# A four-layer image network: when the second layer's Toeplitz matrices are written, which queue loads half of each row tile, and where the next tile is normalized

## The chip, the cores and the metric

The kernel runs on one core of one Trainium2 chip. The metric is the device time of one execution in microseconds (us). Before the change the median of three runs was 6182.19 us (6163.62 to 6187.67).

The engines are named as the profile names them: PE is TensorE (PEld its weight loads), DVE is VectorE, ACT is ScalarE, POOL is GpSimd, SP is SyncE. SP computes nothing here; it issues DMAs. POOL issues DMAs too, among other work. A name with a q (SPq) is an engine's queue of such instructions.

## The reference

An image batch of 8 x 56 x 56 pixels with 192 channels goes through four layers, each with a normalization ahead of it and a residual sum after it. The first two layers are alike and are the ones that the change touches:

```
p = silu(x @ p_w.T + p_b)          # 192 -> 576 channels
q = silu(x @ q_w.T + q_b)
v = silu(x @ v_w.T + v_b)
a1 = rpe_mlp_1(positions) * decay  # one number for each lag and channel
a2 = rpe_mlp_2(positions) * decay
qv = q * v
o1 = toeplitz(qv along the width, a1)
o2 = toeplitz(qv along the height, a2)
y  = (p * (o1 + o2)) @ o_w.T + o_b # 576 -> 192
```

`toeplitz` is a causal and anticausal convolution of 56 positions: for each channel a 56 x 56 matrix whose entry depends on the difference of row and column alone. The third layer is a 7 x 7 depthwise convolution with a two-matrix MLP, the fourth is attention in windows.

## The kernel before, in words

All arithmetic is in float32. The eight samples are taken in pairs (j and j+4 stand together in a tile of 128 partitions), and the pairs in two halves, j0 = 0 and j0 = 2. For each Toeplitz layer and half there are three generators of work, which yield a planned time after each piece:

- `tno_qv` (called Q) projects 128 tokens at a time to q and v (matmuls, L256), adds the bias (DVE, L265), applies Silu (ACT, L275), multiplies (DVE, L278), and stores qv to DRAM through SP (L281). Each group of 256 tokens is loaded two groups ahead (L233) and normalized on ACT (L239). 128 tokens make three pieces of 5.3, 5.3 and 1.3 planned us.
- `tno_toeplitz` (called TZ) does the Toeplitz products. It goes through 18 numbers n = (block of 64 channels, direction d). For each n it loads a tile `q` of qv and a tile `tm` of matrices (L338), both two ahead. For d = 0 the load of `q` comes in two halves, each 56 partitions by 56 rows of 512 bytes (L328); for d = 1 it is one load of long rows (L331). Then come eight groups of products (`along`, L350 on PE, copied from PSUM by ACT at L357) and eight groups of transposes (`turned`, L367 on PE, copied or added by DVE at L370 and L373), and the sum goes to DRAM through POOL (L383). A yield comes after every four groups.
- `tno_out` (called O) does the gate p, the output projection and the residual. It has 28 steps of 224 tokens. A step runs on PE for two tiles at once: the p projection of the tile `now` and the output projection of the tile `before`. Its PSUM tiles are two for the gate (`gs`) and one named `P`, which holds the output projection and, in the same banks, the gate's last 64 channels (`rem`). [...] After the matmuls, ACT applies Silu to `gs` (L511), DVE adds bias and residual out of `P` (L521, L524), POOL stores the result (L117), ACT applies Silu to `rem` (L528), and DVE normalizes the tile `after` for the next step (L449, three instructions). The next step begins with L538, which multiplies by the gates.

`weave` runs a lane of one or two generators and takes pieces of another one between them, in proportion to planned time. When 0.9 of a generator's planned time is done, it calls for the first piece of the next one, which starts its loads; if that next one stands in the next lane, it first gives out all that is left of the pieces taken beside. The lanes are these, and the wall times are read from the profile:

| lane | pieces beside | us |
|---|---|---|
| Q of layer 0, j0 = 0 | matrices of layers 0 and 1 | 0 to 457 |
| Q of layer 0, j0 = 2 | TZ of layer 0, j0 = 0 | 457 to 1108 |
| O of layer 0, j0 = 0; Q of layer 1, j0 = 0 | TZ of layer 0, j0 = 2 | 1108 to 2062 |
| O of layer 0, j0 = 2; Q of layer 1, j0 = 2 | TZ of layer 1, j0 = 0 | 2062 to 3000 |
| O of layer 1, j0 = 0 | TZ of layer 1, j0 = 2 | 3000 to 3560 |
| O of layer 1, j0 = 2 | first half of the depthwise convolution | 3560 to 4190 |

The Toeplitz matrices are made by `expand_tables`: 36 copies for each layer from a small table in DRAM to the 56 x 56 matrices in DRAM, each copy 2048 rows of 224 bytes, issued by SP (L201). They read the table with an overlapping pattern, so that each row is the last one shifted by a position. The first lane begins with 20 of its yields already spent, since `first` is advanced by 20 before the second half's statistics are taken.

In the lanes of TZ the order of instructions on PE, ACT and DVE is the program's order. In the first lane and in the last one a scheduler orders them. SP and POOL take their DMAs in order, and one that has to wait holds up those behind it.

Of the kernel before, what the change touches and what calls it, by code (L numbers as in the profile page):

```python
# [21 lines left out]
B, H, W, C = 8, 56, 56, 192  # L22
# [16 lines left out]
class Net:  # L39
# [275 lines left out]
    def tno_toeplitz(self, j0, mats, qv, o):  # L315
# [3 lines left out]
        nc, p = self.nc, self.tz  # L319
        PR = H // 2  # L320

        def load(n):
            blk, d = divmod(n, 2)
            q = p.tile([128, H, 128], F32, name="q", bufs=2)
            if d == 0:
                for half in range(2):
                    of = qv[2 * blk + half, :T].rearrange("(h w) e -> w h e", w=W)
                    nc.sync.dma_start(q[64 * half : 64 * half + W], of)  # L328
            else:
                of = qv[2 * blk : 2 * blk + 2].rearrange("n (h w) e -> (n h) (w e)", w=W)  # L330
                nc.sync.dma_start(q.rearrange("p i e -> p (i e)"), of)  # L331
            return q
# [60 lines left out]
        for n in range(NS):  # L393
            blk, d = divmod(n, 2)
            q = loaded.pop(0)
# [23 lines left out]
    def tno_out(self, L, j0, xs, gn, o, ys, gn_next, early):  # L419
# [3 lines left out]
        nc, p, inp = self.nc, self.tp, self.inp  # L423
# [22 lines left out]
        def normalize(j, x):  # L446
            xn = p.tile([128, 3, N], F32, name="t4")
            for k in range(3):
                nc.vector.tensor_scalar(  # L449
                    xn[:, k, :], x[:, k, :], gn[:, j, k, 0:1], gn[:, j, k, 1:2], ALU.mult, ALU.add  # L450
                )
            return xn

        def step(now, before, after):
            if now:
                xn, s = now[5], now[3]
# [50 lines left out]
            if now:  # L507
                for i in range(2):
                    pg = p.tile([128, 2, 2, N], F32, name="t4")
                    for c in range(2):  # L510
                        nc.scalar.activation(  # L511
                            pg[:, c],
                            view(gs[i], c * 256, [[512, 2], [1, N]]),
                            AF.Silu,
                            bias=pb[:, 2 * i + c : 2 * i + c + 1],
                        )
                    gates.append(pg)
            if before:
                j, t, x, g, st, _ = before
                y = g[:, 0:3]  # L520
                nc.vector.scalar_tensor_tensor(  # L521
                    y[:, 0:2], P[:, :, :N], ob[:, 0:1], x[:, 0:2], ALU.add, ALU.add
                )
                nc.vector.scalar_tensor_tensor(y[:, 2], po2, ob[:, 1:2], x[:, 2], ALU.add, ALU.add)  # L524
                self.store_pair(ys, j, slice(t * N, (t + 1) * N), y)
            if now:
                pg = p.tile([128, N], F32, name="t1", bufs=1)
                nc.scalar.activation(pg, rem, AF.Silu, bias=pb[:, 4:5])  # L528
                gates.append(pg)
            return normalize(*after) if after else None  # L530

        gates = []

# [18 lines left out]
        if early:  # L552
            yield None
            xn = normalize(j0, x2[:, :, :N])
        yield 0.0
        if not early:
            xn = normalize(j0, x2[:, :, :N])
        done = None
        for n, (j, t) in enumerate(tiles):
# [9 lines left out]
            after = None  # L569
            if n + 1 < len(tiles):  # L570
# [6 lines left out]
                after = tiles[n + 1][0], x2[:, :, at : at + N]  # L577
            xn = step(now, before, after)
# [36 lines left out]
            pass  # L615

    @staticmethod
    def part(gen, t):

        for dt in gen:  # L620
            yield dt
            t -= dt
            if t <= 0:
                return

    def tno_layers(self, x0, x1, x2, gn, last):


        tc, nc = self.tc, self.nc
        LS = ("L0", "L1")  # L630
        tables = [

            [self.dram.tile([D1 + 1, 112], F32, name=f"{L}_tab{d}") for d in range(2)]
            for L in LS
        ]
        mats = [
            [self.dram.tile([D1 // 32, 64, 32 * H], F32, name=f"{L}_mat{d}") for d in range(2)]
            for L in LS
        ]
# [6 lines left out]
        with ExitStack() as ctx, ExitStack() as wqp:  # L646
# [5 lines left out]
            QT, OT, TZT = 25 * 2.25 * 5.3, 28 * 10.7, 8 + 72 * 3.2  # L652

            with tc.tile_pool(name="tab", bufs=2) as tab:
                self.input_stats(x0, gn[0], 0, tab)
                self.decay_tables("L0", tab, tables[0])
                first = Q(0, 0)
                for n in range(20):
                    next(first)
                self.input_stats(x0, gn[0], 2, tab)  # L660
                none = tab.tile([112, 512], F32, name="none", bufs=1)
                nc.gpsimd.memset(none, 0.0)
                for qv in qvs.values():
                    to = qv[:, T:].rearrange("n (p k) e -> p n (k e)", p=112)
                    nc.gpsimd.dma_start(to, view(none, 0, [[0, D1 // 32], [1, 512]]))
                self.decay_tables("L1", tab, tables[1])
                for t in tables:
                    for d in range(2):
                        nc.gpsimd.dma_start(t[d][D1:], none[:1, :112])
                lanes = [[(first, QT)], [(Q(0, 2), QT)], [(O(0, 0), OT), (Q(1, 0), QT)]]  # L670
                lanes += [[(O(0, 2), OT), (Q(1, 2), QT)], [(O(1, 0), OT)], [(O(1, 2, False), OT)]]
                mat = (m for i in range(2) for m in self.expand_tables(tables[i], mats[i]))
                self.weave(lanes[0], mat, lanes[1][0][0], 72.0, 0.0, 0.88)
            in_order = tc.manual_schedule(engines=ENGINES)
            with tc.tile_pool(name="tz", bufs=1) as self.tz, in_order:
                self.tms = []
# [909 lines left out]
```

## Time and profile before

| | us |
|---|---|
| median of three runs | 6182.19 |
| the profiled execution | 6174.82 |
| its span, first to last instruction | 6172.7 |
| PE busy | 5666.5 (92%) |
| weight loads of PE busy | 4464.1 (72%) |
| DVE busy | 2847.8 (46%) |
| ACT busy | 2153.0 (35%) |
| POOL busy | 639.2 (10%) |

Shares of busy time are means over stages. The profile gives for each wait who waited, at which line, and which instruction ended the wait: "PE bank L467 <- DVE t L449" means that PE at line 467, which writes the PSUM tile `bank`, stood idle until DVE at line 449 had written `t`. "issue" is idle time for which the profile shows no wait. In the timeline each line has the start, the length from there to the end of the merged group, the engine, the line, the operation, what it writes and reads, its shape, and how many instructions are merged; a bracket holds the idle time of the engine ahead of it and who ended it.

### The profile page before, as it was taken

The numbers are of one execution on the slowest core, as the hardware profiler recorded it, in microseconds if no ns is written. First come the engines' busy times: TensorE is split into PE (matmuls) and PEld (weight loads), VectorE is DVE, ScalarE is ACT, GpSimd is POOL, SyncE is SP. The second block draws the span as 40 slices with busy tenths as digits, with TensorE's granted clock in tenths as the row PEclk, the third lists the DMA queues.
The fourth block names the chain that finished last, engine by engine and source line by source line (L and its number), as shares of the span: only waits on it lengthen the run. The fifth ranks groups of instructions, "written<-read, shape, count | busy, mean of one in ns | idle before, by whom it ended". The sixth has DMA issues, their size and how long they took to land.

```text
span 6172.7 us, 151914 instructions
## 1 busy us (share of the span) xinstructions
PE 5666.5 (92%) x68832; PEld 4464.1 (72%) x68832; DVE 2847.8 (46%) x4858; ACT 2153.0 (35%) x2736; POOL 639.2 (10%) x833
## 2 busy tenths in 40 slices
PE   4997999899999999999889989999999999988997
PEld 3776878788778788888778878885665444666666
DVE  6663555444556444456444443242221322556555
ACT  1343444223444333344333332224323333333332
POOL 0000000000000000000000010000000100333332
PEclk9998999999999999999999999999999999999998
DMA  7799998887676788776899956663444322344442
GB/s 251 173 207 251 259 249 229 221 241 236 183 206 185 193 239 241 193 212 180 220 247 247 264 171 224 213 221 128 155 163 139 96 63 61 71 87 96 90 90 59
DMA packets 1139557, 1119.75 MB, mean 181 GB/s; under 512 B 342528, under 2 KB 1076736, under 8 KB 1123488
## 3 DMA queue, kind: packets, MB, share of 16 engines
q1 hardware_dynamic: 1103328, 909.05, 54.6%
q0 software_dynamic: 35584, 200.98, 10.4%
q8 instruction: 541, 8.86, 0.6%
q14 instruction: 104, 0.85, 0.0%
HBM read 753.79 MB, written 389.15 MB: 185 GB/s over the span
## 4 chain that ended last, share of the span: by engine, by line
PE 69%; DVE 9%; DMA 4%; ACT 3%; issue 3%; SPq 2%; POOL 1%; POOLq 0%; DVEq 0%; ACTq 0%
PE bank L256 11%; PE bank L350 7%; PE bank L903 6%; PE bank L467 6%; PE bank L477 5%; PE bank L367 5%; PE bank L764 5%; PE bank L983 4%; PE bank L482 3%; PE bank L499 3%; PE bank L997 3%; DMA qv<-t 2%; PE bank L1124 1%; PE bank L1177 1%; POOL e L1229 1%
## 5 line engine op out<-in xcount | busy, mean ns | idle before, releaser
L256 PE MATMUL bank<-wq,t 64*128 64x256 f32 (+5 forms) x8000 | 1319.6, 372 | 62.9 <-ACT t L239 42.8
L256 PEld LDWEIGHTS bank<-wq,t 64*128 64x128 f32 (+3 forms) x8000 | 1040.1, 189 | 313.4 <-issue 115.6
L275 ACT ACTIVATE t<-t 128x2048 f32<-128x2048 f32 (+1 forms) x300 | 444.2, 1488 | 777.9 <-DVE t L265 764.8
L265 DVE TENSOR_TENSOR t<-bank,wq 128x1024 f32<-128x1024 f32 (+2 forms) x500 | 540.2, 1112 | 254.1 <-PE bank L256 253.3
L357 ACT COPY ot<-bank 128x896 f32<-128x896 f32 x576 | 484.3, 920 | 384.6 <-PE bank L350 380.2
L350 PE MATMUL bank<-q,tm 56*64 56x112 f32 x18432 | 521.2, 265 | 64.2 <-issue 44.0
L511 ACT ACTIVATE t<-bank,wo 128x448 f32<-128x448 f32 x448 | 247.9, 635 | 895.3 <-PE bank L482 870.9
L350 PEld LDWEIGHTS bank<-q,tm 56*64 56x64 f32 x18432 | 479.9, 137 | 100.2 <-issue 70.3
L367 PE MATMUL bank<-ident,ot 120*128 120x120 f32 x4032 | 472.9, 276 | 76.8 <-ACT ot L357 37.2
L278 DVE TENSOR_TENSOR t<-t 128x1024 f32<-128x1024 f32 (+1 forms) x300 | 285.1, 955 | 530.8 <-ACT t L275 451.3
L367 PEld LDWEIGHTS bank<-ident,ot 120*128 120x128 f32 x4032 | 431.8, 145 | 125.9 <-ACT ot L357 42.8
L467 PE MATMUL bank<-t,wo 128*128 128x224 f32 x1792 | 393.2, 375 | 45.3 <-DVE t L449 42.3
L903 PE MATMUL bank<-z,w 128*128 128x448 f32 (+1 forms) x1344 | 413.1, 555 | 1.6 <-ACT h L912 1.6
L521 DVE SCALAR_TENSOR_TENSOR t<-bank,wo,t 128x448 f32<-128x448 f32 x112 | 76.4, 682 | 705.6 <-PE bank L506 705.6
L467 PEld LDWEIGHTS bank<-t,wo 128*128 128x128 f32 x1792 | 349.8, 202 | 63.8 <-issue 39.9
L477 PE MATMUL bank<-t,wo 128*128 128x224 f32 x1792 | 363.2, 356 | 11.3 <-issue 6.8
L538 DVE TENSOR_TENSOR t<-t,t 128x896 f32<-128x896 f32 x224 | 235.8, 1083 | 296.2 <-ACT t L511 296.1
L477 PEld LDWEIGHTS bank<-t,wo 128*128 128x128 f32 x1792 | 340.3, 192 | 19.7 <-issue 13.2
L764 PEld LDWEIGHTS bank<-xt,cm 113*112 113x112 f32 x3072 | 309.2, 178 | 36.9 <-issue 30.8
L903 PEld LDWEIGHTS bank<-z,w 128*128 128x128 f32 (+1 forms) x1344 | 182.2, 189 | 205.0 <-issue 196.8
L383 POOL DMA_DIRECT2D L_sum<-s x288 | 141.1, 496 | 1769.1 <-DVE s L373 1766.3
L764 PE MATMUL bank<-xt,cm 113*112 113x108 f32 (+2 forms) x3072 | 317.4, 263 | 4.3 <-ACT h L912 3.2
(142 smaller groups left out, 6940.1 us busy)
## 6 DMA issues: line engine op xcount, KB each, us to landing
q<-qv SPq DMA_DIRECT2D x36, 3584.0 KB
q<-qv SPq DMA_DIRECT2D x72, 1568.0 KB
L_sum<-s POOLq DMA_DIRECT2D x288, 392.0 KB, 7.6
t<-L_sum SPq DMA_DIRECT2D x112, 1008.0 KB
qv<-t SPq DMA_DIRECT2D x192, 512.0 KB
cm<-in_L_cm SPq DMA_DIRECT2D x96, 896.0 KB
tm<-L_mat SPq DMA_DIRECT2D x72, 896.0 KB
x<-t POOLq DMA_DIRECT2D x112, 336.0 KB, 5.5
```

The lines of the kernel that those rows point to most:

```text
L256: nc.tensor.matmul(pp[:m, b, 256 * j : 256 * j + k], x[rows, j, 2 if part else b, s : s + m], w[rows, part, c0 + c : c0 + c + k],  start=p ...
L265: nc.vector.tensor_add(z[:m, c : c + k, :], view(pp[:m], 0, [[1, k], [256, 4]]), view(bias[:m], c0 + c, [[1, k], [0, 4]]),)
L275: nc.scalar.activation(z[:m, :n, :], z[:m, :n, :], AF.Silu)
L278: nc.vector.tensor_mul(prod[:m, :k], half[:, :, 0], half[:, :, 1])
L350: nc.tensor.matmul(pt[64 * s : 64 * s + 64, r, j * 112 : (j + 1) * 112], tm[rows, c * H : c * H + 64], q[rows, PR * s : PR * s + PR, 4 * c ...
L357: nc.scalar.copy(view(ot, 4 * g, [[112 * 32, 2], [32, 112], [1, 4]]), view(pt, 0, [[512, 2], [1, 112], [112, 4]]),)
L367: nc.tensor.transpose(pz[:, i, :120], ot[:120, at : at + 128], self.ident[:120, :120])
L467: mm(gs[c // 2][:, b, c % 2 * 256 : c % 2 * 256 + N], pw[:, 0, 128 * c : 128 * c + 128], xn[:, b], start=c % 2 == 0, stop=False,)
L477: mm(P[:, b, :N], ow[:, c, 0:128], g[:, 4 * b + c], start=c == 0, stop=False)
L511: nc.scalar.activation(pg[:, c], view(gs[i], c * 256, [[512, 2], [1, N]]), AF.Silu, bias=pb[:, 2 * i + c : 2 * i + c + 1],)
L764: nc.tensor.matmul(pc[:, 128 * e + 4 * m0 : 128 * e + 4 * m1], cm[:113, e, k, :], xt[:, m0 - 1 + k : m1 - 1 + k, c + e, :], start=n == 0 a ...
L903: nc.tensor.matmul(phs[c][:, s, :TT], w0[rows, part, at : at + 128], z[rows, Z[2 if part else s], :], start=part == flip, stop=part != flip,)
```

## The change

There are three edits.

1. The first lane's pieces beside are the matrices of layer 0 alone (36 copies, planned 36.0), and its planned length is 71 less. The matrices of layer 1 are taken two by two after each of the first 18 steps of the first O, by a new helper `beside`.
2. For d = 0 the second half of the load of `q` is issued by POOL (`nc.gpsimd`), the first by SP as before.
3. In a step of O, `normalize(*after)` stands ahead of the evictions L521 and L524, in place of behind everything.

```diff
@@ tno_toeplitz, load
-                for half in range(2):
+                for half, queue in enumerate((nc.sync, nc.gpsimd)):
                     of = qv[2 * blk + half, :T].rearrange("(h w) e -> w h e", w=W)
-                    nc.sync.dma_start(q[64 * half : 64 * half + W], of)
+                    queue.dma_start(q[64 * half : 64 * half + W], of)
@@ tno_out, step
                     gates.append(pg)
+            xn = normalize(*after) if after else None
             if before:
                 j, t, x, g, st, _ = before
...
-            return normalize(*after) if after else None
+            return xn
@@
+    def beside(gen, other, n):
+
+        for dt in gen:
+            for i in range(n if dt else 0):
+                next(other, None)
+            yield dt
+        for more in other:
+            pass
@@ tno_layers
-                lanes = [[(first, QT)], [(Q(0, 2), QT)], [(O(0, 0), OT), (Q(1, 0), QT)]]
+                lanes = [[(first, QT - 71.0)], [(Q(0, 2), QT)], [(O(0, 0), OT), (Q(1, 0), QT)]]
                 lanes += [[(O(0, 2), OT), (Q(1, 2), QT)], [(O(1, 0), OT)], [(O(1, 2, False), OT)]]
-                mat = (m for i in range(2) for m in self.expand_tables(tables[i], mats[i]))
-                self.weave(lanes[0], mat, lanes[1][0][0], 72.0, 0.0, 0.88)
+
+                more = self.expand_tables(tables[1], mats[1])
+                lanes[2][0] = (self.beside(lanes[2][0][0], more, 2), OT)
+                mat = self.expand_tables(tables[0], mats[0])
+                self.weave(lanes[0], mat, lanes[1][0][0], 36.0, 0.0, 0.88)
```

More of the change, by code (lines that the diff above doesn't have):

```diff
@@ L617, in part @@
     @staticmethod
+    def beside(gen, other, n):
[5 more added lines that the diff above has]
+            pass
+    @staticmethod
     def part(gen, t):
```

## The prediction

> **What bounds the kernel now.** I read the table by stage first, then the waits of TensorE (PE), then the timeline around each place that an edit touches. The stages below are the lanes of the weaving loop. They begin and end where the last q/v projection or the last output step ends on PE. The columns are length, busy time and count of each engine, granted PE clock, DMA share and GB/s.
>
> ```profile
> core 0: us, PE busy (x) PEld busy (x) DVE busy (x) ACT busy (x) POOL busy (x), PEclk, DMA share, GB/s
> 0.00:457.00 457.00, 367.87 (x2160) 288.50 (x2160) 279.56 (x505) 150.07 (x159) 11.18 (x47) 0.97 0.83 211
> 457.00:1108.00 651.00, 565.74 (x7621) 484.37 (x7617) 329.98 (x349) 266.79 (x297) 34.78 (x72) 0.94 0.93 243
> 1108.00:1580.00 472.00, 444.84 (x5202) 388.53 (x5200) 218.00 (x393) 141.69 (x221) 37.91 (x60) 0.98 0.83 231
> ...
> 2062.00:2540.00 478.00, 455.11 (x5326) 398.31 (x5327) 215.87 (x395) 147.39 (x230) 37.92 (x60) 0.97 0.82 231
> ...
> 3000.00:3560.00 560.00, 500.35 (x7121) 446.49 (x7121) 238.79 (x388) 177.51 (x255) 50.07 (x87) 0.95 0.92 253
> ```
>
> PE is busy for 90 to 95% of every stage after the first. So a microsecond in which PE stops is a microsecond of the end, and a microsecond of DVE, ACT or DMA is worth nothing until it stops PE. DMA is second: 0.93 and 0.92 in the two stages where the row and column products have only one lane beside them, 0.83 where two share them.
>
> The end of the first lane is the largest single stop:
>
> ```profile
> 457.56 0.68 DVE L265 TENSOR_TENSOR t<-bank,wq 64x512 f32<-64x512 f32 x1
> 463.81 24.66 SPq L201 DMA_DIRECT2D L_mat<-L_tab  x11
> 488.59 4.08 SPq L233 DMA_DIRECT2D t<-in_x  x3
> 495.92 3.06 ACT L239 ACTIVATE t<-t,gn 128x256 f32<-128x256 f32 x6 [36.28 <-DMA t<-in_x]
> 496.58 15.65 PE L256 MATMUL bank<-wq,t 128*128 128x256 f32 x76 [39.38 <-ACT t L239]
> ```
>
> Eleven matrix copies left over are issued in a row, the next lane's tokens come behind them, and PE stands for 39.38 us. The window inside it shows the clock and the DMA engines:
>
> ```profile
> 464.00:489.00 25.00, 0.00 (x0) 0.00 (x0) 0.00 (x0) 0.00 (x0) 0.00 (x0) 0.50 1.28 197
> ```
>
> One output projection step, the usual case, with the piece that follows it:
>
> ```profile
> 1309.18 3.23 PE L350 MATMUL bank<-q,tm 56*64 56x112 f32 x124
> 1309.40 0.68 DVE L521 SCALAR_TENSOR_TENSOR t<-bank,wo,t 128x448 f32<-128x448 f32 x1 [9.09 <-PE bank L506]
> 1310.01 0.44 DVE L524 SCALAR_TENSOR_TENSOR t<-bank,wo,t 128x224 f32<-128x224 f32 x1
> 1310.36 1.22 DVE L449 TENSOR_SCALAR t<-t,gn 128x224 f32<-128x224 f32 x3
> 1310.56 0.45 ACT L528 ACTIVATE t<-bank,wo 128x224 f32<-128x224 f32 x1 [3.04 <-DVE t L524]
> 1310.91 3.32 ACT L357 COPY ot<-bank 128x896 f32<-128x896 f32 x4
> 1311.50 2.08 DVE L538 TENSOR_TENSOR t<-t,t 128x896 f32<-128x896 f32 x2
> ```
>
> The reader is to see the order on ACT: L528 waits for the eviction L524, and the four copies of the next piece wait behind L528. Who waits on PE, from 1108 to 3560 us and in the dense stage before it:
>
> ```profile
> PE bank L467 <- DVE t L449: 33.6, 7, 10.0
> ...
> PE bank L350 <- issue: 16.1, 13, 3.5
> ```
> ```profile
> PE bank L350 <- issue: 26.6, 10, 5.4
> ```
>
> And what POOL pays for a DMA of 384 rows and one of 32, with SP's stop behind a pair of row loads:
>
> ```profile
> L117 POOL DMA_DIRECT2D x<-t x112: 744/773/869, 1138.3 to 4188.1; - x112
> L383 POOL DMA_DIRECT2D L_sum<-s x288: 489/489/536, 580.7 to 3609.8; - x144
> 1192.88 10.94 SPq L338 DMA_DIRECT2D tm<-L_mat  x1
> ```
>
> [...] POOL's DMA issues here stay within 0.1 us of their median, [...]
>
> **Edit 1, the matrices.** In the first lane 36 copies remain instead of 72. The lane's length is now right (QT less 71, since 20 of its yields are spent before): all 36 are issued at 0.88 of it, and at 0.9 the next lane's first tokens are called for. Seventeen units of the lane are left then, some 19 us at 13.2 us for 11.9 units (1319.6 us of L256 over 100 token tiles). So the tokens land under work. What is late next: the last Silu (ends at 459.6), then the first normalization (0.58 us), so about 3 us of gap stay. The half clock goes too: the window of 497 to 503 us, when PE works again, still has a granted clock of 0.54, so about half of those 6 us, 3 us, is lost. Saved: 39.4 - 3 + 3 = 39 us. Bounds: 33 (the clock is not regained) to 42. Elsewhere in the lane nothing is gained: PE is busy 50.00 of 50 us in each window from 250 to 450.
>
> The other 36 copies move into the first 18 of 28 steps of the first output projection, two behind each step, on SP's queue ahead of that step's row, column and tm loads. A copy costs 24.66/11 = 2.24 us of a full DMA system, 36 cost 81 us, in some 300 us (18 steps of 16.9). The DMA share there, 1163 to 1463, is 0.81. With 1.04 (500 to 560 us, all loads queued) taken as full, 243/1.04 + 81 = 315 us of transfer in 300. That is over, by 15 us at the end of 18 steps. The loads have more slack than that: s is asked for more than a step (16.9 us) ahead, the row tiles one and a half of the 18 loads ahead, and a load lasts 53 us here (954 us for 18). What has no slack is what the trace calls issue: stops of PE with no wait, 31 us (26.6 + 4.6) in 611 us of the dense stage, few in this one. I take two thirds of that density over 300 us, +10 us. Bounds: 0 and +36 (the 15 counted at full, plus 15 of issue, plus 6 for half clock).
>
> **Edit 2, half a row load on POOL.** 36 loads of 3136 rows of 512 B. From 32 rows 0.489 us and 384 rows 0.773 us, 0.81 ns a row: 3.0 us each, 109 us of POOL, which is busy 19 to 50 us in each of these stages. Its stores L117 and L383 are issued after PE has passed the piece that the load waits for, so little stands behind it. SP is blocked a few us less 36 times, [...] I take 0. Bounds: -15 (half of the 32 us in which PE waits for L265, late through DVE's wait for qv stores) and +45 (rival below).
>
> **Edit 3, the normalization first.** L449's three come before L521 and L524, which end 1.14 us later (1310.36 to 1311.50), and so does L528. The tile P of PSUM is the third of a step, and four tiles go round: the fourth tile after it takes its banks. Behind a row-product piece that is its fourth group. PE reaches it at about 1311.3 (four groups from 1308.8 to 1312.4), L528 ends at 1311.01: 0.3 us of slack, the same in nearly all such steps. So PE stops for 1.14 - 0.3 = 0.8 us. I counted, in the timelines of the three stages, 41 steps with such a piece behind them and 34 with a transposing piece. The first: 28 in PE-bound stages x 0.8 = 22, 13 in the dense last one at 1.1 (ACT's eight copies run in a chain there) less 30% already lost to waits = 10, and 0.3 x 6 where a transpose follows at once = 2. The 34: DVE's evictions (0.89 a group against PE's 0.72) already hold PE from the fifth group on, so the stop is swallowed; 2 us. Gained: seven steps with no piece between wait 1.55 us for L449, and the first of three would come 1.0 us sooner: -7. The rest of the 33.6 us is DMA at a stage's first step, and stays. In the last output projection DVE has L449 ahead of L521 already. Sum +29; bounds -7 (the stop is absorbed) and +45.
>
> **Sum.** -39 + 10 + 0 + 29 = 0 us. The profiled execution took 6174.82 us for a span of 6172.7; the runs' median is 6182.19, 7 us above it. Likeliest: no change, 6183 us.
>
> **Rivals.** *The eviction stop costs nothing* (PE's later waits for ACT, 29.4 us in all, take it up): -39 + 10 - 7 = -36, 6146 us. For it: such waits exist. Against: most PE-bound windows have hardly any idle time. *The copies overload DMA in the first projection*: +36 in place of +10, 6209. For it: 315 in 300. Against: the first lane ran such copies at shares near 1 with PE at 50.00. *The POOL queue slows the dense stages* (the slower side): [...] Their issue stops (26.6 + 15.6 = 42) double, and 3 us of POOL time come before a load: +45, 6228. It decides from 1.25 us a load on (45/36). Against: slack of the loads.
>
> **How the numbers follow.** Chances: no change 0.43, stop absorbed 0.22, overload 0.15, POOL 0.20. One measurement tells about 0.5%, 31 us, from no change. Faster: two thirds of the second and a sixth of the first, 0.22. Slower: most of POOL, half of the overload, a fifth of the first, 0.35. Same: 0.43. Range 6130 to 6245: the second case less 16, POOL plus 17; the likeliest alone 6150 to 6215.
>
> **What would show it.** Right: the L239 wait at the first lane's end is under 6 us; the fourth group of pieces behind a step starts about 0.8 us later, with PE waiting for L528; DMA share near 1.05 at the first projection's start. Wrong: a second lane still behind copies, stops of PE on q loads, or DVE's L521 ending no later.

## The result and the profile after

| | before | after |
|---|---|---|
| median, us | 6178.32 (4 runs, 6163.62 to 6187.67) | 6232.43 (4 runs, 6224.91 to 6238.18) |
| ratio to before, 95% interval | | 1.0078 [1.0059, 1.0097] |
| span of the profiled execution, us | 6172.7 | 6223.1 |

The change makes the kernel 0.78% slower, 48 us of 6178. The range held it. The likeliest case, no change, did not come: the slowdown is clear of the 0.5% that I had named as the bound of telling. In the comparisons below, two runs in a slower state are left out of the ratios: one of the kernel without copies (6613.76 us at a granted clock of 0.84) and one of the kernel before (24717.51 us at 0.69).

To find the place, I cut each profile where PE takes up a lane's first matmul (L256 for a Q, L467 for an O), and for O(1,0) at the last Toeplitz matmul. All kernels of the later sections stand here too, so that the reader can come back to it. Lengths are in us. "Rest" is what comes after, up to the last matmul.

| kernel | first lane | second lane | O(0,0) | Q(1,0) | O(0,2) | Q(1,2) | O(1,0) | rest |
|---|---|---|---|---|---|---|---|---|
| before | 402.0 | 611.4 | 483.8 | 458.0 | 484.6 | 450.7 | 620.6 | 2560.6 |
| after | 357.5 | 652.2 | 506.7 | 447.3 | 499.1 | 450.3 | 635.3 | 2573.2 |
| edit 1 alone | 360.5 | 651.7 | 488.9 | 450.3 | 484.7 | 452.0 | 621.2 | 2568.5 |
| edit 2 alone | 411.2 | 610.7 | 499.3 | 445.2 | 497.3 | 457.0 | 633.5 | 2565.9 |
| edit 3 alone | 402.4 | 619.0 | 493.8 | 446.5 | 492.3 | 453.6 | 638.1 | 2584.5 |
| edit 1, copies on ACT's queue | 360.7 | 613.1 | 543.3 | 451.7 | 484.2 | 450.9 | 625.5 | 2571.9 |
| copies held until Q(1,0) | 359.8 | 611.3 | 486.5 | 476.1 | 485.6 | 458.7 | 619.9 | 2568.2 |
| no copies for layer 1 | 361.0 | 615.6 | 487.1 | 450.2 | 484.6 | 454.4 | 621.5 | 2559.7 |
| all copies in the first lane | 375.2 | 621.0 | 484.6 | 450.0 | 484.4 | 455.0 | 621.6 | 2566.3 |
| edit 2 without first loads | 401.8 | 628.2 | 483.6 | 444.6 | 483.8 | 445.3 | 625.7 | 2571.3 |
| edit 3 in some steps | 399.8 | 619.8 | 482.4 | 457.3 | 481.5 | 454.9 | 625.3 | 2565.2 |
| Silu of L528 first | 402.9 | 625.7 | 490.3 | 451.2 | 488.0 | 449.8 | 617.4 | 2581.3 |
| gains together, two | 375.6 | 629.7 | 486.3 | 444.6 | 483.9 | 448.6 | 621.0 | 2571.8 |
| gains together, three | 372.7 | 626.8 | 483.2 | 441.2 | 480.9 | 445.0 | 618.4 | 2578.4 |

Each row is one execution. The second lane reads 611 to 626 in kernels that do not touch it, Q(1,0) 445 to 458, O(1,0) 620 to 626, the rest 2560 to 2578. I use a difference only where it is larger than that, or where a wait in the trace names it.

Three things changed. The first lane lost its gap (-44). The second lane took nearly all of it back (+41). Each of the three output projections beside Toeplitz pieces is 15 to 23 longer.

The first view of the kernel after is the table by stage, cut at its own lane starts; its first three stages are shown. The columns are length, busy time and count of PE, PEld, DVE, ACT and POOL, then PE clock, DMA share and GB/s:

```profile
core 0: us, PE busy (x) PEld busy (x) DVE busy (x) ACT busy (x) POOL busy (x), PEclk, DMA share, GB/s
94.10:451.60 357.50, 343.06 (x2080) 270.69 (x2080) 239.24 (x354) 141.00 (x143) 4.54 (x17) 0.97 0.80 198
451.60:1103.80 652.20, 575.75 (x7620) 493.23 (x7616) 326.79 (x346) 264.11 (x291) 49.32 (x81) 0.95 0.93 245
1103.80:1610.50 506.70, 460.39 (x5356) 402.18 (x5352) 217.34 (x401) 146.84 (x229) 46.98 (x66) 0.95 0.79 219
```

The first two of these stages in the kernel before:

```profile
94.50:496.50 402.00, 347.71 (x2080) 272.57 (x2080) 240.82 (x357) 140.92 (x141) 4.52 (x17) 0.92 0.89 199
496.50:1107.90 611.40, 565.45 (x7616) 484.32 (x7616) 326.15 (x343) 263.78 (x295) 34.78 (x72) 0.97 0.91 246
```

So the second lane is longer in two ways. PE stands idle 76 us in it where it stood 46, and it is busy 10 us longer with the same matmuls, at a granted clock of 0.95 where it was 0.97.

The DMA share of O(0,0) is 0.79, no more than before's 0.82. I had expected about 1.05 there, from 36 more copies. They are not there. The view of the copies' line says where they are; its columns are shortest, median and longest issue in ns, then the first and last start:

```profile
L201 SPq DMA_DIRECT2D L_mat<-L_tab x72: 532/600/15502, 136.0 to 723.0; - x72
```

All 72 copies are issued by 723 us, 381 us before O(0,0) begins. In the program's text the second 36 stand between steps of O(0,0). But PE, ACT and DVE alone keep the program's order, and a copy waits for nothing but its table. So SP got them as early as it could, between the loads and stores of the second lane. There the timeline of the kernel after shows what they do to PE (lines of other work are left out):

```profile
554.98 13.89 SPq L281 DMA_DIRECT2D qv<-t  x2
...
568.92 13.94 SPq L201 DMA_DIRECT2D L_mat<-L_tab  x3
...
580.60 1.23 DVE L278 TENSOR_TENSOR t<-t 128x1024 f32<-128x1024 f32 x1 [9.46 <-DMA qv<-t]
581.74 0.68 DVE L265 TENSOR_TENSOR t<-bank,wq 128x512 f32<-128x512 f32 x1
582.48 1.66 PE L367 MATMUL bank<-ident,ot 120*128 120x120 f32 x7 [9.82 <-DVE t L265]
```

SP stands 13.94 us over three copies. DVE's L278 can't write its buffer until a store of qv has read it, and waits 9.46 us for that store. L265, which evicts PSUM, is queued behind L278 on DVE, and PE waits 9.82 us for L265. DVE's waits for stores of qv in this lane, first after (457 to 1104 us), then before (500 to 1108 us):

```profile
DVE t L278 <- DMA qv<-t: 112.9, 15, 14.8
```
```profile
DVE t L278 <- DMA qv<-t: 32.9, 7, 8.4
```

PE's waits from 1108 to 3600 us give the rest:

```profile
PE bank L467 <- DVE t L449: 66.8, 7, 21.9
...
PE bank L350 <- ACT t L529: 11.9, 37, 0.6
PE bank L367 <- ACT t L529: 10.3, 32, 0.6
```

The first was 33.6 us before: it doubled, in as many waits. The two on L529 (before: L528) are new, 69 short ones. L449 belongs to the start of a projection; here is that of O(0,0) in the kernel after:

```profile
1107.93 0.34 SPq L328 DMA_DIRECT2D q<-qv  x1
1108.63 1.58 POOL L328 DMA_DIRECT2D q<-qv  x1 [28.62 <-PE bank L482]
...
1110.21 4.90 SPq L281 DMA_DIRECT2D qv<-t  x2
...
1115.15 15.10 SPq L443 DMA_DIRECT2D t<-L_sum  x2
...
1131.81 1.01 DVE L449 TENSOR_SCALAR t<-t,gn 128x224 f32<-128x224 f32 x3 [19.85 <-DMA qv<-t]
...
1132.35 4.98 PE L467 MATMUL bank<-t,wo 128*128 128x224 f32 x16 [21.95 <-DVE t L449]
```

And the same place in the kernel before:

```profile
1112.68 5.38 SPq L281 DMA_DIRECT2D qv<-t  x2
...
1118.11 3.67 SPq L443 DMA_DIRECT2D t<-L_sum  x2
...
1123.45 1.01 DVE L449 TENSOR_SCALAR t<-t,gn 128x224 f32<-128x224 f32 x3 [9.03 <-DMA qv<-t]
1123.95 0.97 SPq L328 DMA_DIRECT2D q<-qv  x1
1124.00 4.81 PE L467 MATMUL bank<-t,wo 128*128 128x224 f32 x16 [9.98 <-DVE t L449]
```

Before, the second half of q was issued at 1123.95, behind the last stores of qv and behind s and x. After, POOL issues it at 1108.63, ahead of them. The stores land later, and L449 comes 19.85 us late instead of 9.03.

Last, an output step in the kernel after, with a row-product piece behind it:

```profile
1320.52 2.47 PE L350 MATMUL bank<-q,tm 56*64 56x112 f32 x92
1320.73 1.01 DVE L449 TENSOR_SCALAR t<-t,gn 128x224 f32<-128x224 f32 x3 [9.40 <-PE bank L503]
1321.65 0.68 DVE L522 SCALAR_TENSOR_TENSOR t<-bank,wo,t 128x448 f32<-128x448 f32 x1
...
1322.80 0.45 ACT L529 ACTIVATE t<-bank,wo 128x224 f32<-128x224 f32 x1 [3.94 <-DVE t L525]
...
1323.30 1.00 PE L350 MATMUL bank<-q,tm 56*64 56x112 f32 x32 [0.31 <-ACT t L529]
```

L449's three take 0.92 us to the start of what follows, and L529 waits 3.94 us where L528 waited 3.04. PE's first group starts at 1320.15 (a few matmuls ahead of the first line), and its fourth, the last 32 matmuls, 3.15 us later. In the step shown with the prediction, the fourth group started 2.57 us after the first. The stop is 0.58 us long, of which the trace shows 0.31 as a wait.

### The profile page after: what moved, and what is told of

It reads as the page before. It is cut to its first block, busy times and chain, and to the rows that moved or that the text cites. A ratio compares the mean times of both kernels' runs of the same rounds, so it can differ in the third digit from the quotient of the medians.

```text
span 6223.1 us, 151993 instructions
## 1 busy us (share of the span) xinstructions
PE 5674.7 (91%) x68832; PEld 4473.7 (72%) x68832; DVE 2835.2 (46%) x4858; ACT 2149.9 (35%) x2736; POOL 696.0 (11%) x869
## 5 line engine op out<-in xcount | busy, mean ns | idle before, releaser
L256 PE MATMUL bank<-wq,t 64*128 64x256 f32 (+5 forms) x8000 | 1313.4, 371 | 27.4 <-issue 12.7
L256 PEld LDWEIGHTS bank<-wq,t 64*128 64x128 f32 (+3 forms) x8000 | 1037.6, 188 | 274.1 <-issue 115.8
L265 DVE TENSOR_TENSOR t<-bank,wq 128x1024 f32<-128x1024 f32 (+2 forms) x500 | 539.3, 1111 | 178.9 <-PE bank L256 178.6
L357 ACT COPY ot<-bank 128x896 f32<-128x896 f32 x576 | 482.4, 922 | 379.7 <-PE bank L350 374.9
L350 PE MATMUL bank<-q,tm 56*64 56x112 f32 x18432 | 521.2, 264 | 83.4 <-issue 44.6
L367 PE MATMUL bank<-ident,ot 120*128 120x120 f32 x4032 | 487.9, 281 | 97.3 <-ACT ot L357 44.2
L350 PEld LDWEIGHTS bank<-q,tm 56*64 56x64 f32 x18432 | 474.7, 136 | 124.5 <-issue 74.4
L278 DVE TENSOR_TENSOR t<-t 128x1024 f32<-128x1024 f32 (+1 forms) x300 | 284.6, 955 | 591.6 <-ACT t L275 433.7
L367 PEld LDWEIGHTS bank<-ident,ot 120*128 120x128 f32 x4032 | 446.9, 149 | 145.8 <-ACT ot L357 49.8
L467 PE MATMUL bank<-t,wo 128*128 128x224 f32 x1792 | 389.2, 372 | 78.3 <-DVE t L449 76.8
L449 DVE TENSOR_SCALAR t<-t,gn 128x224 f32<-128x224 f32 x336 | 113.0, 393 | 755.6 <-PE bank L503 691.8
L467 PEld LDWEIGHTS bank<-t,wo 128*128 128x128 f32 x1792 | 347.8, 201 | 94.9 <-issue 71.2
L370 DVE COPY s<-bank 128x784 f32<-128x784 f32 x288 | 259.2, 963 | 89.2 <-PE bank L367 51.7
```

The source lines that it names most:

```text
L256: nc.tensor.matmul(pp[:m, b, 256 * j : 256 * j + k], x[rows, j, 2 if part else b, s : s + m], w[rows, part, c0 + c : c0 + c + k],  start=p ...
L265: nc.vector.tensor_add(z[:m, c : c + k, :], view(pp[:m], 0, [[1, k], [256, 4]]), view(bias[:m], c0 + c, [[1, k], [0, 4]]),)
L278: nc.vector.tensor_mul(prod[:m, :k], half[:, :, 0], half[:, :, 1])
L350: nc.tensor.matmul(pt[64 * s : 64 * s + 64, r, j * 112 : (j + 1) * 112], tm[rows, c * H : c * H + 64], q[rows, PR * s : PR * s + PR, 4 * c ...
L357: nc.scalar.copy(view(ot, 4 * g, [[112 * 32, 2], [32, 112], [1, 4]]), view(pt, 0, [[512, 2], [1, 112], [112, 4]]),)
L367: nc.tensor.transpose(pz[:, i, :120], ot[:120, at : at + 128], self.ident[:120, :120])
```

## The experiments

### One edit at a time

The kernel before with edit 1 alone, edit 2 alone and edit 3 alone: the diffs are the three parts shown above. Expected were:

> Edit 1 alone. Theory (the moved copies do not wait for their place in the program, SP issues them in the second lane, at 480 to 725 us): the 39 us stop at the end of the first lane goes, the second lane takes about 35 us more, total -4, 6174 us. Rival (the second lane is slow because of the row halves on POOL): the copies cost nothing there, total -39, 6140 us, and the second lane takes 611 us as before.

> Edit 2 alone. Theory (POOL's half overtakes the last qv stores and first loads at the three starts of an output projection, each start stops PE 12 us longer): +36, 6214 us, with the longest L467 waits near 21 us in place of 9, and the second lane at 611 us. Rival (POOL also slows the second lane by 35 us): +71, 6250 us.

> Edit 3 alone. Theory (PE waits for L528's successor about 0.3 us in some 70 steps, and saves 1 us in 7 steps): +15, 6193 us. Rival (the stop is 0.8 us behind each row-product piece, as was forecast): +29, 6207 us. Second rival (nothing): 6178 us.

| alone | median, us | ratio to before (6186.88) | us by ratio |
|---|---|---|---|
| edit 1 | 6183.64 | 0.9991 [0.9980, 1.0002] | -5 |
| edit 2 | 6209.9 | 1.0039 [1.0027, 1.0051] | +24 |
| edit 3 | 6225.43 | 1.0053 [1.0035, 1.0070] | +33 |

The sum is +52 where the whole change measured +48. Each of these numbers is uncertain by 7 to 12 us, and within that the edits add.

Edit 1 came as expected. It gains its gap and loses it again in the second lane (360.5 and 651.7 in the table).

Edit 2 costs 24 us (interval 17 to 32) where 36 were expected, and in the places expected, the starts of the three projections. PE's waits for L449 from 1108 to 3600 us were 33.6 us before:

```profile
PE bank L467 <- DVE t L449: 70.9, 7, 21.7
```

There is a fourth place, which I had not expected. At the end of the first lane POOL issues the half of the first q while SP still has its eleven copies to issue:

```profile
462.88 33.89 SPq L201 DMA_DIRECT2D L_mat<-L_tab  x11
465.19 1.60 POOL L328 DMA_DIRECT2D q<-qv  x1 [243.19 <-DMA qv<-t]
```

The copies took 24.66 us before, and PE's stop there is 48.8 us instead of 39.4 (first lane 411.2 in the table). In the whole change these copies are gone from that place, so this part of the loss is not in its +48.

For edit 3 the expectation of +15 missed, and its rival, the +29 of the prediction, was about right: the interval is +22 to +43. The size was right; where it comes from is tested below.

### Edit 1 with the copies in the place where the text has them

The 36 copies of layer 1 are issued by ACT, which keeps the program's order. The diff is against edit 1 alone.

```diff
-    def expand_tables(self, tables, mats):
+    def expand_tables(self, tables, mats, queue=None):
...
-                self.nc.sync.dma_start(mat[n].rearrange("p (c w) -> p c w", w=H), src)
+                (queue or self.nc.sync).dma_start(mat[n].rearrange("p (c w) -> p c w", w=H), src)
...
-                more = self.expand_tables(tables[1], mats[1])
+                more = self.expand_tables(tables[1], mats[1], nc.scalar)
```

> Edit 1 with the 36 moved copies issued by ACT, whose order is the program's, so that they stay in the first output projection. Theory: gap gone, second lane 611 us, +10 us in the first output projection: -29, 6149 us. Rival (copies are dear wherever they run): like e1_only, 6174 us. If ACT is held up by its own copies, PE waits for ACT and it is slower than e1_only.

6196.61 us, ratio 1.0017 [1.0008, 1.0025]. The second lane is back at 613.1, and O(0,0) is at 543.3. So it was the copies that made the second lane long, and they went there because SP's order is not the text's. But this is no better place, for a second reason:

```profile
L201 ACTq DMA_DIRECT2D L_mat<-L_tab x36: 528/1836/11830, 1084.6 to 1415.9; - x36
```
```profile
PE bank L467 <- ACT ot L357: 27.7, 6, 8.2
```

The median issue takes 1.84 us of ACT and the longest 11.83. The copies out of PSUM (L357) stand behind them on ACT, and PE waits for those.

### What do the copies cost, and is there a place where they are free?

My theory by now: the copies are dear only because they fall into the second lane, where the DMA engines have no room. Three kernels test it. All have the corrected length of the first lane, and differ in what they do with the second 36. The first reads them from a copy of the tables that ACT writes in program order at the start of Q(1,0), so that SP cannot issue them before. A helper like `beside` gives out one copy behind every second piece of Q(1,0):

```diff
...
-                mat = (m for i in range(2) for m in self.expand_tables(tables[i], mats[i]))
-                self.weave(lanes[0], mat, lanes[1][0][0], 72.0, 0.0, 0.88)
+                late = [self.dram.tile([D1 + 1, 112], F32, name=f"late{d}") for d in range(2)]
+
+                def held():
+                    flat = lambda t: bass.AP(t.tensor, t.offset, [[4039, 16], [1, 4039]])
+                    for d in range(2):
+                        nc.scalar.dma_start(flat(late[d]), flat(tables[1][d]))
+                    yield from self.expand_tables(late, mats[1])
+
+                lanes[2][1] = (self.beside(lanes[2][1][0], held()), QT)
+                mat = self.expand_tables(tables[0], mats[0])
+                self.weave(lanes[0], mat, lanes[1][0][0], 36.0, 0.0, 0.88)
```

> The kernel before with the first part of the change, but the 36 copies of the second layer's matrices cannot be issued early: they read a copy of the tables that ACT writes in program order at the start of the second layer's q/v projection (1590 us), and come one behind every second piece there. My theory, that the first part gained nothing because SP issued these copies into the second lane: the 39 us gap at 457 is gone, the second lane is back at 611 us (652 with the first part alone), the q/v projection Q(1,0), where the DMA engines are at 0.7, gets 0 to 10 us longer; total 30 to 40 us below the kernel before, about 6150. Rival, that 36 such copies cost some 40 us wherever they run: Q(1,0) at 490 us instead of 450, total as before, about 6185.

The second has edit 1's shorter first lane and leaves the second 36 copies out; layer 1 then reads layer 0's matrices:

```diff
-            TZ = lambda i, j0: self.tno_toeplitz(j0, mats[i], qvs[j0], o[i])
+            TZ = lambda i, j0: self.tno_toeplitz(j0, mats[0], qvs[j0], o[i])
...
```

> The first part of the change without the 36 copies of the second layer's matrices (the second layer's row and column products then use the first layer's matrices, so that part of the computation is left out). Whatever this is faster than the first part alone (6184) is the full price of the 36 copies there. My theory, that they cost what the gap's removal gains: second lane 611 us instead of 652, total 6140 to 6150. Rival, that the second lane is long for another cause (the lane's changed end, shifted phases): second lane stays near 650, total about 6180.

The third leaves all 72 in the first lane and corrects its length alone:

```diff
-                lanes = [[(first, QT)], [(Q(0, 2), QT)], [(O(0, 0), OT), (Q(1, 0), QT)]]
+                lanes = [[(first, QT - 71.0)], [(Q(0, 2), QT)], [(O(0, 0), OT), (Q(1, 0), QT)]]
```

> The kernel before with the corrected length of the first lane alone: all 72 matrix copies stay in the first lane, none is left over at its end. My theory, that the copies were hidden in the first lane already and only those left over cost anything: gap at 457 gone, first lane 360 to 370 us, second lane 611 to 616, total 30 to 55 below the kernel before (the kernel with the second layer's copies left out is 57 below it). Rival, that the first lane has no room for all 72 within 0.88 of its length: first lane 15 us or more longer than with 36, or copies run on into the second lane, total within 15 us of before.

Measured, with the price of the 36 copies as the ratio less that of the kernel without them (0.9907), times 6187 us. Two intervals of about 0.0012 to either side make each price uncertain by some 11 us.

| where the 36 copies run | median, us | ratio to before | price, us |
|---|---|---|---|
| nowhere | 6129.44 | 0.9907 [0.9893, 0.9920] | 0 |
| first lane, SP | 6164.35 | 0.9974 [0.9961, 0.9988] | 41 |
| second lane, SP (edit 1 alone) | 6183.64 | 0.9991 [0.9980, 1.0002] | 52 |
| O(0,0), ACT | 6196.61 | 1.0017 [1.0008, 1.0025] | 68 |
| Q(1,0), SP | 6173.52 | 0.9974 [0.9964, 0.9985] | 41 |

That the copies are what edit 1 gives back holds: without them the second lane is at 615.6 and the gain is 57 us. But the theory that they are dear only in the second lane fell. I had put 0 to 10 us on them in Q(1,0), and they cost 41; its rival, "some 40 us wherever they run", had it right. SP issued these copies from 1539.4 to 1863.8 us. Q(1,0) is 476.1 us long with them, and the table by stage has a DMA share of 0.85 where edit 1 alone has 0.68:

```profile
1550.00:2050.00 500.00, 450.28 (x4624) 376.07 (x4624) 270.04 (x283) 206.17 (x225) 19.38 (x40) 0.94 0.85 216
```

PE there waits for L265 by 38.5 us, in the kernel with held copies (three lines, 1540 to 2017 us):

```profile
PE bank L367 <- DVE t L265: 18.5, 3, 15.7
PE bank L350 <- DVE t L265: 11.3, 2, 10.9
PE bank L256 <- DVE t L265: 8.7, 1, 8.7
```

With edit 1 alone it waits 13.5 us for L265 in the same projection. And DVE's L278 waits 55.0 us for stores of qv, with edit 1 alone 20.1. So the path is that of the second lane again: copies, the store of qv, L278, L265, PE. A mean share of 0.68 did not mean that a store had room.

The third kernel halves my expectation as well (-16 us by ratio; I had said 30 to 55). The gap is gone, yet the first lane is 375.2 against the 360.5 with 36 copies in it, and the second lane 621.0. Its rival had said 15 us or more, and 14.7 came. That is not all of the 41 us: the second lane has some 5 more than without the copies, and the rest is not placed by the table. The copies' line shows SP held twice as long by each:

```profile
L201 SPq DMA_DIRECT2D L_mat<-L_tab x72: 527/1129/6177, 136.5 to 456.8; - x72
```

### Is it the first load that costs in edit 2?

```diff
-                for half in range(2):
+                for half, queue in enumerate((nc.sync, nc.gpsimd if n > 1 else nc.sync)):
```

> The second part of the change, except that the first load of q in each of the three row-and-column stages keeps both halves on SP. My theory, that the second part costs 24 us because at the start of each output projection GpSimd's half overtakes the last stores of qv and the first loads of the output step: these starts are as before (first L449 of the stage waits about 9 us for DMA, not 20), total within 8 us of the kernel before (6187). Rival, that the loads on GpSimd slow the stages throughout: 6205 to 6211, as with the whole second part.

6181.98 us, ratio 0.9988 [0.9977, 0.9999], -7 us. PE's waits for L449 are as before (34.5 us in 7 where edit 2 alone has 70.9), and O(0,0), O(0,2) and O(1,0) are at 483.6, 483.8 and 625.7.

The expectation speaks of three stages, but the edit puts back four halves, the first of each of the four TZ, and the stop at the first lane's end is back at 39.3 us too. Four halves of a load, each issued while another lane ends, are the whole loss of edit 2. The other 32 cost nothing in the total that can be told. They may move time: the second lane reads 627 to 630 in the three kernels that have only these on POOL, above all others without added copies, and Q(1,0) 441 to 445.

### Which steps does edit 3 cost in?

The normalization goes ahead of the evictions only in steps that have a transposing piece or no piece behind them, by a list of step numbers read from the timeline of before. The 41 steps with a row-product piece behind and the last projection keep the old order.

```diff
+            if ahead and after:
+                xn = normalize(*after)
             if before:
...
-            xn = step(now, before, after)
+            xn = step(now, before, after, early and n not in rows)
```

> The third part of the change in those steps alone that have a transposing piece or no piece behind them (in the three output projections beside row and column products; 41 steps with a row-product piece behind keep the order of before, and so does the last projection). My theory, that the third part costs where PE takes a fourth PSUM group 2.6 us after the step, and there alone: 0 to 15 us below the kernel before. Rival, that later evictions on DVE and ACT cost in every step (the stops add up to 24 of 33 us only): 8 to 18 us above before.

6178.8 us, ratio 0.9993 [0.9984, 1.0002]. The later eviction is there in these steps as well, and PE waits for the Silu behind it 33 times:

```profile
PE bank L367 <- ACT t L534: 10.7, 33, 0.6
```

The total shows no cost of it (-4 us, interval -10 to +1), as the first expectation had it; the rival of 8 to 18 us fell. That DVE's evictions of the transposes hold PE in the same piece anyway, as the prediction argued (0.89 us a group against PE's 0.72), fits, but no run separates it.

What is left for the 33 us are the steps with a row-product piece behind and the last projection, and the traces tell these apart. In the last projection DVE takes L449 ahead of L521 before (3925.41 and 3927.34 us) as well as with edit 3 alone (3958.74, then L522 at 3960.67). It lasts 587.5 us with edit 3 alone, and 579 to 589 us in the kernels that leave it as it was. So the cost is in the steps with a row-product piece behind. The length of "rest" with edit 3 alone (2584.5) is for the most part from work behind the last projection, which no edit touches (1997 us, before 1979).

In the three projections, edit 3 alone and edit 3 in some steps differ in these 41 steps only, by 11.4, 10.8 and 12.8 us. I measure a step from its first L467 to the next one's. In the first two projections 26 such steps can be compared. With edit 3 alone 22 of them are longer by 0.55 us in the mean, and the other four by 2.4 to 2.6 us. In these four, transposes follow the row products at once. Here they are in the first of the four, with edit 3 in some steps, then with edit 3 alone, and the last line is the window of the latter:

```profile
1232.90 3.09 PE L367 MATMUL bank<-ident,ot 120*128 120x120 f32 x28 [1.86 <-ACT ot L357]
```
```profile
1238.69 4.75 PE L367 MATMUL bank<-ident,ot 120*128 120x120 f32 x28 [2.22 <-ACT ot L357]
1238.69:1243.28 4.59, 4.59 (x29) 4.59 (x29) 2.46 (x3) 0.00 (x0) 0.00 (x0) 0.63 0.98 403
```

PE waits 0.36 us longer for ACT's copies, whose start the later Silu has put off. So these steps lose some 0.9 us for certain. The other 1.66 us are clock: behind the wait it is 0.63, where with edit 3 in some steps it stays at 1.00 (1232.9 to 1235.8 us), and the same 28 transposes take longer. That this is the edit's doing is not shown. With edit 3 alone the clock falls in all four places, in the whole change in two, before in one, and with edit 1 alone in two, behind a wait of 1.86 us as before.

### Would an earlier Silu help?

If L528's lateness is what stops PE, the Silu of the half tile can go ahead of DVE's evictions.

```diff
+                pg = p.tile([128, N], F32, name="t1", bufs=1)
+                nc.scalar.activation(pg, rem, AF.Silu, bias=pb[:, 4:5])
+                gates.append(pg)
             if before:
...
-            if now:
-                pg = p.tile([128, N], F32, name="t1", bufs=1)
-                nc.scalar.activation(pg, rem, AF.Silu, bias=pb[:, 4:5])
-                gates.append(pg)
```

> The kernel before with ACT's L528, the Silu on the half tile, emitted ahead of DVE's two evictions L521 and L524, so that it waits for PE alone. ACT is then free 1.3 us earlier behind each step (it waits 3.04 us for L524 now). If ACT's lateness is what stops PE behind a step, the fourth group of the piece behind a step comes no later and the time is 0 to 20 us less; if the tile P is released by L524 on DVE at the same time as before, the time is the same (6187 within 5 us). That is the likelier, since PE hardly stops there before.

Neither came: 6209.9 us, ratio 1.0038 [1.0025, 1.0051]. The timeline shows that the eviction now waits for the Silu:

```profile
1331.29 0.45 ACT L519 ACTIVATE t<-bank,wo 128x224 f32<-128x224 f32 x1 [1.88 <-issue]
1331.77 0.68 DVE L524 SCALAR_TENSOR_TENSOR t<-bank,wo,t 128x448 f32<-128x448 f32 x1 [9.62 <-ACT t L519]
```

ACT and DVE both read the tile P of PSUM here and neither writes it, yet they go one after the other: DVE starts 0.03 us after ACT ends. In the kernel before, with the two the other way round, ACT's L528 waits 3.04 us for DVE's L524 and starts 0.11 us after its end (1310.45 and 1310.56 us, in the step shown with the prediction). What makes them take turns is not shown. So P comes free no earlier: its last reader ends 2.17 us after the first matmul of the piece behind the step, where it ended 2.20 us after it before. And DVE's own work comes some 0.5 us later. Whether that makes the 23 us is not shown. The profiled execution has them in "rest" for the most part (2581.3 in the table), but its last projection lasts 579.7 us, no longer than before (581.2), and the work behind that is not touched by the edit.

### The parts that gain, together

With the corrected lane length and edit 2 without the first loads:

> The corrected lane length with all copies in the first lane, and the second part of the change without the first load of each stage. If the parts add, as the three of the change did (-5 + 24 + 33 for 48 measured): the corrected lane's gain and a further 0 to 10 us, some 45 to 65 below before. If the load on GpSimd only moves time (the q/v projections 5 to 13 us shorter, the second lane 17 longer where it was alone): the corrected lane's gain alone.

With edit 3 in some steps besides:

> All three: the corrected lane length with the copies in the first lane, GpSimd's half without each stage's first load, and the normalization ahead of the evictions in the steps without a row-product piece behind. If parts add, the sum of the three gains, 45 to 75 us below before; if the third part costs in all steps, 8 to 18 above the kernel with the first two.

6154.7 us, ratio 0.9953 [0.9936, 0.9971], and 6153.97 us, ratio 0.9952 [0.9939, 0.9966]. The sum of the measured parts is -16 -7 = -23 for the first and -27 for the second; they measured -29 and -30. So the first beats the kernel before by 0.47% [0.29, 0.64], and the whole change by 1.0078 - 0.9953 = 1.25%, some 77 us. What edit 3 in some steps adds to it cannot be told from nothing. Both are short of the 45 us that I had put at the least, since the corrected lane brings 16 and not 30 or more.

## Why the prediction was right or wrong

**What bounds the kernel** held in the main: the losses found begin with stops of PE, and a stop of PE was a stop of the end. It was not the whole: PE also lost busy time at a lower granted clock (10 of the 41 us in the second lane, at 0.95 where it was 0.97), which the prediction counted for the gap and in a bound, not in its likeliest sum.

**Edit 1, the gap.** The mechanism was right: no L239 wait is left at the first lane's end. The lane is 44 us shorter in the whole change and 41.5 with edit 1 alone, where 39 was said (bounds 33 to 42). Of the 44 us, 40 are idle time and 4.65 busy time (347.71 to 343.06 us), for which the prediction had 3.

**Edit 1, the copies.** Here the first step failed: "The other 36 copies move into the first 18 of 28 steps of the first output projection, two behind each step, on SP's queue ahead of that step's row, column and tm loads." The program's text has them so. I had written myself that the order held is that of PE, ACT and DVE, and did not draw the conclusion for SP: a copy with no wait was issued as early as SP would have it, here in the second lane, the last at 723 us. That is the case "a second lane still behind copies", which stands in the prediction as a sign of being wrong. The second fault is in the price of +10 us. I weighed the 36 copies' 81 us of transfer against the loads, whose slack I had measured, and took only "issue" stops as a cost. The transfer without slack was the store of qv, on which DVE's L278 waits (112.9 us in the second lane, 32.9 before) and behind it L265. The runs give 41 to 68 us in every place tried; none is near +10, and the lowest, with its uncertainty of 11, is 30. The overload rival (+36) had nearly the size, in the wrong stage and for the wrong wait. So edit 1 was worth -5 us, not -29.

**Edit 2.** The step that failed is "I take 0", an estimate made without a row load on POOL in any trace. For the steady loads it was right (edit 2 without the first loads: -7 us, POOL's issue 1.57 us for a load where I had taken 3.0). I had looked at what stands behind POOL's issue and at what SP gains, but not at what the load is issued *ahead of*. At three starts it overtakes the last stores of qv and the first s and x of the output step, and PE waits some 12 us longer at each (70.9 - 33.6 = 37 us in sum with edit 2 alone). With edit 2 alone it also overtakes the copies left over in the first lane, 9 us more. These stops make 46 us in the profiled execution, the slowest of its ten; by the ratio of all runs edit 2 costs 24, and where the difference comes back is not shown. That the order does the harm is read from the timelines; a first half issued by POOL behind the stores was not tried. The rival of the slower side, "The POOL queue slows the dense stages", whose issue stops were to double, was an estimate. It gave the right sign by another mechanism, and its mark fell: the issue stops of L350 in the dense second lane are 25.1 us after and 26.6 before, and 32.5 with edit 2 alone is no more than the 32.0 with edit 1 alone, which has no row load on POOL. Also 1.57 us a load lies above the 1.25 from which it was to decide, and the steady loads cost nothing.

**Edit 3.** The mechanism held: the stop lies at the fourth group behind a row-product piece, PE waits there for the Silu, and behind transposes it costs nothing in the total. The last projection, put at nothing, costs nothing that can be told. The size came out by luck, since terms were mis-sized in both directions. The usual stop is 0.55 to 0.58 us, not 0.8, since L449's three cost 0.92 ahead of the evictions, not 1.14. Against that, "0.3 x 6 where a transpose follows at once = 2" was too little: four such steps lost 0.9 us each, and 1.66 more each at a lower clock. In the first two projections that makes 22 us for 26 steps (22 x 0.55 + 10), where 22 was said for 28 from a stop of 0.8. In the dense stage the difference is 12.8 us where 10 was said, in a stage that scatters by 6. The gain was counted in seven steps of 1.55 us. But three of the seven waits for L449 are those for DMA at a stage's start, 27.4 of the 33.6 us, so only four steps had 1.55 us to lose. Each of these four gained what was said for one (1.55 us at 1138.42 us before, 0.58 at 1146.44 with edit 3 alone). That makes -4 us, not -7. In sum +33 [+22, +43] stands against +29 (bounds -7 and +45).

**Sum.** -29 + 0 + 29 was said, -5 + 24 + 33 measured, +48 for all. Two terms missed by 24 us each in the same direction. That the range held the result is luck: it reached that far for the rival of the POOL queue, whose mechanism did not come.

## What to carry to other kernels

Before an instruction is moved by moving its line in the program, ask which engines keep the program's order: here copies that wait for nothing ran where SP's queue got to them, 381 us and more before the place of their text. For a transfer that is added or put forward, look for the transfer with the least slack, here the store of qv that must leave its buffer, and follow who waits for it (DVE's waits for it rose from 32.9 to 112.9 us in the second lane); a mean DMA share of 0.68 hid that in Q(1,0). And a second queue did more here than issue a load in 1.57 us: ask what the load now overtakes, above all where one lane ends and the next begins (PE waited some 12 us longer at each of three such places). Last, take each wait of a sum one by one: of the seven waits for L449 three had another cause, 27.4 of the 33.6 us, and the mean hid it.

## What the runs showed of the hardware

- The price of 36 copies did not fall with the DMA share of their stage: 41 us where the share without them is 0.68 (Q(1,0)), and 41 to 52 where it is 0.80 and 0.90 (first and second lane).
- In the kernel after, SP kept a matrix copy, for which the profile shows no wait, behind a store of qv that had to wait for DVE: it issued nothing for 4.52 and 4.31 us ahead of two such stores (L281, at 410.93 and 449.48 us), and the copy behind each 0.06 and 0.05 us after it.
- In these runs a DMA issue held its engine far longer than its usual time when other transfers had been issued ahead of it: on SP 15.10 us for two loads of s behind POOL's half, which took 3.67 before, and up to 11.83 us for one copy on ACT (median 1.84). ACT's copies out of PSUM stood behind these, and PE waited 27.7 us for them.
- POOL issued a load of 3136 rows in 1.57 us (1.547 to 1.598), half of the 3.0 us to which a line through 32 and 384 rows (0.489 and 0.773 us) had led me.
- After a stop of PE the granted clock could be lower: 0.54 in the first 6 us behind the 39 us gap, and 0.63 over 4.6 us behind a wait of 2.22 us (28 transposes took 4.75 us instead of 3.09). Behind waits of 1.86 and 2.22 us in the same four places it fell in some executions and not in others.
- Two engines that only read one PSUM tile ran one after the other in the steps shown: DVE began 0.03 us after ACT ended with the Silu first, and ACT 0.11 us after DVE ended in the kernel before. There the order of the two readers moved the wait and did not take it away.
